# Moving the last sequence's gated experts into the scans of the next block

## The chip, the cores and the metric

The kernel runs on one core of a Trainium2 chip as one launch. The metric is the device time in microseconds, as the median of several executions. TensorE (PE), VectorE (DVE), ScalarE (ACT), GpSimd (POOL) and SyncE (SP, which here issues most DMAs) work from queues of their own and wait for each other by semaphores.

## The reference

Eight sequences of 512 tokens of 128 features (float32) go through four layers, each an attention part and a feed-forward part with a residual. The change touches where the third layer's feed-forward part (gated experts) meets the fourth layer's attention part (a state-space scan). What matters:

```python
# L2 ffn: 32 experts of 64 units, 4 of them chosen for each token
gates = sigmoid(xt @ expert_sel.T); gate_full = gates of the 4 largest, else 0
scores = relu(einsum('nd,edf->nef', xt, keys)) * gate_full[:, :, None]
out = einsum('nef,efv->nv', scores, values)          # added to x
# L3 attn: for each of 16 heads, 8 channels and 48 states
h = exp(dt_t * A) * h + (dt_t * u_t) * b_t           # along the 512 tokens
y_t = sum over states of h * c_t
```

After the scan there are an output projection, a gated MLP (`silu(gate) * up`, then `down`), and the last layer's feed-forward part with spiking units.

## The kernel before

`NB = 8` sequences, `S = 512` tokens, `P = D = 128`. The residual `X[b]` of all sequences stays in SBUF (four tiles of 128 tokens each). The function `l2_attn_l3_attn` (from L1072) holds both stages that matter.

*Expert stage* (L1626 to L1667). For each sequence `b` it runs 16 steps `j` of two experts. A step multiplies the normalised, transposed sequence `xT` with two experts' keys into PSUM (`key`, L1644), VectorE takes the maximum with 0 and multiplies with the gates (`act`, L1648, gates spread over 64 partitions each by DMA, `fetch_gates`, L1397), and three steps later TensorE multiplies with the values and accumulates (`acc`, L1622). After 16 steps `give_back` (L1408) copies, transposes and adds the sum to `X[b]` and takes the statistics for the next norm. Beside these steps run, one piece at each step, the generators in `side`: `route` (router of the next sequence), `banded` (attention of the one after) and twice `prepare`. In the last sequence's 16 steps, the fifth also issues the first loads of the scans (`fetch`, `fetch_dt`, L1656 to L1660).

*Scan stage* (L1860 to L1911). For each sequence there are four row blocks `q` and three state groups `g`: a *group* in the text is one (b, q, g), of which a sequence has 12. A group does, twice (`j` = 0, 1): two matmuls `bx` (L1879) from `gx`, an exponential `a` on ScalarE (L1885), and the scan `h` on VectorE (L1890). `bx` has two PSUM buffers, `a` four buffers. The group's output matmuls `Z` (`give`, L1690) follow one group later. `gx` is loaded by four DMAs (L1313, three buffers) and multiplied in place with `xk` by GpSimd (`products`, L1335). Beside the groups, one piece each, run the generators in `side`: `prepare(b + 2)` (L1227: norm, convolution, step size with a polynomial for log(1+z) on GpSimd, L1271 to L1292), `project(b - 1)` (L1703: projection and MLP, with GpSimd's L1727 and L1732 ahead of the transposes at L262) and late in the stage `layer_3b`. They share two PSUM buffers (`mm_tile`, L1101).

The order of the text is not quite the order of the queues: when the program is built, the tile framework puts the instructions of each engine into one list, which the engine then follows. What is called "the built program" below is this list.

Of the kernel before, what the change touches and what calls it, by code (L numbers as in the profile page):

```python
# [16 lines left out]
F32 = mybir.dt.float32  # L17
BF16 = mybir.dt.bfloat16
AF = mybir.ActivationFunctionType
ALU = mybir.AluOpType  # L20
# [3 lines left out]
P = 128  # L24
NB = 8
S = 512
C = S // P
D = 128
# [39 lines left out]
def eight_layers(ctx: ExitStack, tc: tile.TileContext, w: dict, out: bass.AP):  # L68
    nc = tc.nc

    const = ctx.enter_context(tc.tile_pool(name="const", bufs=1))
# [40 lines left out]
    X = [xpool.tile([P, C, D], F32, tag=f"x{b}", name=f"x{b}") for b in range(NB)]  # L112
# [9 lines left out]
    later = []  # L122
# [6 lines left out]
    def square(name, put=load):  # L129
        return put(name, [P, P], w[name])  # L130
# [43 lines left out]
    f1_sg = load_later("L1_ffn_shared_gate_w", [P, 512], w["L1_ffn_shared_gate_w"])  # L174
# [3 lines left out]
        w["L1_ffn_shared_down_w"].rearrange("(k p) d -> p k d", p=P),  # L178
    )

    a2 = {k: square(f"L2_attn_{k}", load_later) for k in ("WQ", "WK", "WV")}
    f2_sel = load_later("L2_ffn_expert_sel", [P, 32], w["L2_ffn_expert_sel"])
    f2_k = load_later("L2_ffn_keys", [P, 32, 64], w["L2_ffn_keys"].rearrange("e d f -> d e f"))
    f2_v = load_later(
# [55 lines left out]
    def cols(c):  # L240
        return slice(c * P, (c + 1) * P)

    def stats(b, mv, x=None):

        x = X[b] if x is None else x
        for c in range(C):
            st = small.tile([P, 6], F32, tag="bn", name="bn", bufs=4)
            nc.vector.bn_stats(st, x[:, c, :])  # L248
            nc.vector.bn_aggr(mv[:, b * C + c, :], st)
# [822 lines left out]
    def l2_attn_l3_attn():  # L1072
# [15 lines left out]

        E = 32
        J = E // 2  # L1090
        G = 3
        Q = 4
        with ExitStack() as es:
# [7 lines left out]
            def mm_tile():  # L1101
                return ps.tile([P, S], F32, tag="mm", name="mm")
# [24 lines left out]
            def step(gens):  # L1127
                for g in list(gens):
                    if next(g, None) is None:
                        gens.remove(g)  # L1130
# [93 lines left out]
            x1 = {}  # L1224
            rows = {}

            def prepare(b, fine=False):  # L1227
# [5 lines left out]
                nc.gpsimd.tensor_tensor(rr, rr, mv3[:, tiles(b), 1], ALU.mult)  # L1233
                nc.gpsimd.tensor_scalar(rr, rr, 1e-6, None, ALU.add)
                nc.gpsimd.tensor_tensor(rr, rr, minus_half[:, 0:C], ALU.pow)
                xn = work.tile([P, C, D], F32, tag="x1", name="x1", bufs=NB)
                normal(b, mv3, r, xn)
                x1[b] = xn
                yield True
# [98 lines left out]
            with ExitStack() as es2:  # L1338
# [25 lines left out]
                def route(b):  # L1364
                    r = rstd_of(mv2, b, b == 0)
                    yield True
                    xn = ffn.tile([P, C, D], F32, tag="xn", name="xn")
                    normal(b, mv2, r, xn)
                    yield True
                    xT = ffn.tile([P, S], F32, tag="xT", name="xT")  # L1370
                    flipped(xn, mm_four(), xT)
                    yield True
                    lp = mm_four()[:, :, 0:E]
                    for c in range(C):
                        nc.tensor.matmul(lp[:, c, :], xT[:, cols(c)], f2_sel, start=True, stop=True)
                    gt = ffn.tile([P, C, E], F32, tag="gt", name="gt")
                    nc.scalar.activation(gt, lp, AF.Sigmoid)
                    yield True
                    full = first_max(gt, False)
                    for k in range(1, 4):  # L1380
                        yield True
                        oh = first_max(gt, k == 3)
                        nc.vector.tensor_tensor(full, full, oh, ALU.add)
                    yield True
                    mm = mm_four()
                    for c in range(C):
                        nc.tensor.transpose(mm[0:E, c, :], full[:, c, :], ident)
                    gT = ffn.tile([E, S], F32, tag="gT", name="gT", bufs=1)
                    nc.scalar.copy(gT, mm[0:E].rearrange("p c t -> p (c t)"))
                    gd = dram.tile([E, S], F32, tag="gates", name="gates", bufs=3)  # L1390
                    nc.sync.dma_start(gd, gT)
                    ready[b] = xT, gd
                    yield True
# [229 lines left out]
                    if j == J - 1:  # L1623
                        side.append(give_back(b, acc))

                for b in range(NB):  # L1626
                    xT = ready[b][0]
                    if b < NB - 1:
                        side.append(route(b + 1))
                    if b < NB - 2:  # L1630
                        side.append(banded(b + 2))
                    if b < NB - 3:
                        gather(b + 3)
                    acc = ps2.tile([P, S], F32, tag="acc", name="acc", bufs=2)
                    for j in range(J):
                        if j % 2 == 0:
                            m = 8 * b + j // 2 + 3
                            if m < 8 * NB:
                                while m // 8 not in ready:
                                    step(side)  # L1640
                                fetch_gates(m // 8, m % 8)
                            gate = spread.pop((b, j // 2))
                        key = ps2.tile([P, S], F32, tag="key", name="key", bufs=3)
                        nc.tensor.matmul(  # L1644
                            key, f2_k[:, 2 * j : 2 * j + 2, :], xT, start=True, stop=True
                        )
                        act = ffn.tile([P, S], F32, tag="act", name="act", bufs=5)
                        nc.vector.scalar_tensor_tensor(  # L1648
                            act, key, 0.0, gate[:, j % 2, :], ALU.max, ALU.mult
                        )  # L1650
                        if len(sums) > 2:
                            add_up()
                        sums.append((b, j, act, acc))
                        if j == 4 and b in (NB - 5, NB - 3):
                            side.append(prepare((b - NB + 5) // 2, True))
                        if j == 4 and b == NB - 1:  # L1656
                            nc.vector.tensor_copy(late, act[:, 0:2])
                            fetch(0, 0)
                            fetch_dt(0, 0)
                            fetch(0, 1)  # L1660
                        if j == 12 and b == NB - 1:
                            products(0, 0)
                        step(side)
                while sums:
                    add_up()
                while side:
                    step(side)  # L1667


            with ExitStack() as es2:  # L1670
# [32 lines left out]
                def project(b, zx):  # L1703
# [59 lines left out]
                    given.add(b)  # L1763
                    yield True

                order = [(b, q) for b in range(NB) for q in range(Q)]

                inputs = {}
# [2 lines left out]
                def layer_3b(b, tail):  # L1771
# [51 lines left out]
                            yield True  # L1823
                    y = o.rearrange("p c d -> p (c d)")
                    if b < NB - 1:
                        y = work.tile([P, S], F32, tag="x1", name="x1", bufs=NB)
                        nc.scalar.copy(y, o.rearrange("p c d -> p (c d)"))
                    inputs[b] = y
                    yield True
# [27 lines left out]
                    nc.gpsimd.dma_start(out[b].rearrange("(c p) d -> p c d", p=P), X[b])  # L1857
                    yield True

                side = []  # L1860
                n = 0
                for b in range(NB):
                    if b < NB - 2:
                        side.append(prepare(b + 2))
                    for q in range(Q):
# [7 lines left out]
                        for g in range(G):  # L1873
                            hs = []
                            for j in range(2):
# [16 lines left out]
                                    bx.rearrange("p r t -> p (r t)"), 0.0, ALU.mult, ALU.add,  # L1892
                                )
                                hs.append(h)
                            made.append((b, q, g, hs, xk))
                            if len(made) > 1:
                                give()
# [87 lines left out]
```

## Time and profile before

| | us |
|---|---|
| median of 3 runs (lowest, highest) | 1713.37 (1712.08, 1717.24) |
| the profiled execution, its own time | 1725.08 |
| its span from first to last instruction | 1723.3 |
| busy: TensorE, VectorE, ScalarE, GpSimd | 1470.0, 1206.9, 796.6, 677.8 |
| experts of the last sequence, from the first of its value matmuls to the last | 1098.1 to 1122.8 |
| first scan starts | 1129.8 |
| granted TensorE clock, mean | 0.935 |

An engine's row in the timeline gives start and duration in us, engine, line, operation, tiles, shapes and, in brackets, the idle time before and who ended it. A matmul of float32 appears as two records. In a row of stretches, each engine has its busy time and (in brackets) its number of instructions, followed by TensorE's clock, the DMA engines' busy share and GB/s. In the waits, each line says which line of which engine waited for which, for how long in total, how often, and the longest. The chain of waits is followed back from the last instruction.

### The profile page before, as it was taken

Reading aid. Unit: us, or ns where it says so; the run is one execution under the profiler, and the core shown is the slowest. Engines: PE = TensorE matmul, PEld = TensorE weight load, DVE = VectorE, ACT = ScalarE, POOL = GpSimd, SP = SyncE. Lnnn points to the kernel's source line nnn. Section 1 sums busy time; section 2 is a strip of 40 time slices with the busy share of each in tenths; the row PEclk is TensorE's granted clock in tenths of the full one; section 3 lists DMA queues with packets and bytes.
Section 4 is the critical chain, followed back from the end, with each engine's and each line's share of the span. In section 5 each row is a group of like instructions: output and inputs, shape, how many; then the busy total and the mean of one; then the engine's idle time right before and its main releaser. Section 6 shows DMA issues by size and latency. Waiting matters only on the chain.

```text
span 1723.3 us, 22463 instructions
## 1 busy us (share of the span) xinstructions
PE 1470.0 (85%) x8060; PEld 651.2 (38%) x8061; DVE 1206.9 (70%) x2374; ACT 796.6 (46%) x1158; POOL 677.8 (39%) x728
## 2 busy tenths in 40 slices
PE   5978898899888868988999896977888888888887
PEld 2322333334344435644555453422222222233335
DVE  7688666655654444357775764589899999988765
ACT  3655655555454423353223230055555565565634
POOL 4754344443321140211213318135645645712750
PEclk8999899999899889988999898999899999999988
DMA  7991000000000022304544653634444444443201
GB/s 270 384 342 34 1 1 13 7 13 13 13 19 19 13 99 78 95 10 109 124 116 118 134 126 95 151 80 129 124 127 128 133 129 125 131 117 95 61 13 31
DMA packets 94224, 164.69 MB, mean 96 GB/s; under 512 B 10848, under 2 KB 36960, under 8 KB 90016
## 3 DMA queue, kind: packets, MB, share of 16 engines
q1 hardware_dynamic: 89392, 151.97, 31.4%
q0 software_dynamic: 3568, 9.18, 1.7%
q10 hardware_dynamic: 1152, 2.10, 0.4%
q8 instruction: 64, 1.05, 0.3%
q14 instruction: 48, 0.39, 0.1%
HBM read 110.27 MB, written 52.95 MB: 95 GB/s over the span
## 4 chain that ended last, share of the span: by engine, by line
PE 43%; DVE 28%; issue 10%; POOL 7%; ACT 5%; DMA 5%; SPq 1%; DVEq 0%; POOLq 0%; ACTq 0%
DVE h L1890 11%; PE key L1644 5%; PE acc L1622 5%; PE bx L1879 3%; DMA gx<-du_d 2%; PE mm L262 2%; PE sT L568 2%; DVE mf L547 2%; PE o L591 2%; PE sc L536 1%; PE gu L369 1%; PE gu L1055 1%; DMA gate<-gates 1%; DVE zx L1698 1%; PE Z L1690 1%
## 5 line engine op out<-in xcount | busy, mean ns | idle before, releaser
L1890 DVE TENSOR_TENSOR_SCAN h<-a,bx 128x1024 f32<-128x1024 f32 x192 | 426.9, 2269 | 29.2 <-PE bx L1879 27.7
L1885 ACT ACTIVATE a<-dr,nA 128x1022 f32<-128x1022 f32 x192 | 219.4, 1146 | 221.2 <-DVE h L1890 221.0
L1879 PE MATMUL bx<-gx,wb 64*128 64x512 f32 x768 | 220.2, 666 | 61.3 <-DVE h L1890 59.2
L1335 POOL TENSOR_TENSOR gx<-gx,xk 128x1024 f32<-128x1024 f32 x32 | 75.4, 2357 | 226.0 <-DMA gx<-du_d 194.3
L1644 PE MATMUL key<-xT,L_ffn_keys 128*128 128x512 f32 x256 | 136.4, 615 | 22.9 <-DVE act L1648 22.9
L1879 PEld LDWEIGHTS bx<-gx,wb 64*128 64x128 f32 x768 | 64.8, 195 | 195.1 <-DVE h L1890 149.8
L1622 PE MATMUL acc<-act,L_ffn_values 128*128 128x512 f32 x256 | 132.7, 602 | 0.0
L1648 DVE SCALAR_TENSOR_TENSOR act<-key,gate 128x512 f32<-128x512 f32 x128 | 86.5, 685 | 47.8 <-PE key L1644 34.6
L1690 PE MATMUL Z<-h,wc 64*32 64x512 f32 x1536 | 110.3, 628 | 0.1
L547 DVE TENSOR_REDUCE mf<-sm 128x8 f32<-128x1024 f32 x64 | 76.1, 1211 | 42.5 <-POOL sm L543 42.4
L577 POOL TENSOR_SCALAR_AFFINE_SELECT eT<-eT 128x1024 f32<-128x1024 f32 x64 | 68.9, 1099 | 78.7 <-ACT eT L575 78.7
L543 POOL TENSOR_SCALAR_AFFINE_SELECT sm<-sm 128x1024 f32<-128x1024 f32 x64 | 69.4, 1098 | 71.2 <-ACT sm L542 70.9
L1433 POOL DMA_INDIRECT back<-f_out,back_at x32 | 30.8, 964 | 155.7 <-DVE bn L248 139.3
L542 ACT COPY sm<-sc 128x1024 f32<-128x1024 f32 x64 | 62.5, 1014 | 54.7 <-PE sc L536 40.6
L1410 ACT COPY oT<-acc 128x512 f32<-128x512 f32 x8 | 4.7, 587 | 159.2 <-PE acc L1622 159.2
L575 ACT ACTIVATE eT<-sT 128x1024 f32<-128x1024 f32 x64 | 62.0, 1021 | 28.0 <-PE sT L568 27.9
L1644 PEld LDWEIGHTS key<-xT,L_ffn_keys 128*128 128x128 f32 x256 | 47.1, 195 | 73.2 <-issue 36.2
L1622 PEld LDWEIGHTS acc<-act,L_ffn_values 128*128 128x128 f32 x256 | 49.1, 193 | 60.0 <-issue 60.0
L536 PE MATMUL sc<-kb,qT 32*128 32x512 f32 x256 | 58.9, 724 | 10.0 <-ACT sm L542 4.1
L248 DVE BATCH_NORM_STATS2 bn<-x 128x6 f32<-128x128 f32 x224 | 56.1, 272 | 4.8 <-DMA x<-in_L_attn_hidden_states 4.0
L1116 POOL TENSOR_TENSOR rstd<-rstd,minus_half 128x4 f32<-128x4 f32 x27 | 28.0, 1040 | 80.0 <-DVE rstd L1115 79.8
L568 PE MATMUL sT<-qT,kb 32*128 32x512 f32 x256 | 55.2, 655 | 4.5 <-ACT sm L542 2.9
(482 smaller groups left out, 3006.4 us busy)
## 6 DMA issues: line engine op xcount, KB each, us to landing
f_in<-zeros SPq DMA_DIRECT2D x10, 3584.0 KB
gate<-gates SPq DMA_DIRECT2D x128, 256.0 KB
dr<-dt_d SPq DMA_DIRECT2D x32, 1024.0 KB
gx<-du_d SPq DMA_DIRECT2D x128, 128.0 KB
xk<-xh_d SPq DMA_DIRECT2D x32, 256.0 KB
wide<-in_L_ffn_experts SPq DMA_DIRECT2D x1, 3072.0 KB
xg<-f_in SPq DMA_DIRECT2D x48, 64.0 KB
f_out<-ys SPq DMA_DIRECT2D x12, 256.0 KB
```

The lines of the kernel that those rows point to most:

```text
L536: nc.tensor.matmul(halves[q // 2][:, 4 * (q % 2) : 4 * (q % 2) + 4, :], qT[quad(q), cols(c)], kb[quad(q)], start=True, stop=True,)
L543: nc.gpsimd.affine_select(out=sm, in_=sm, compare_op=ALU.is_ge, fill=-1e30, base=0, pattern=[[0, 8], [-1, P]], channel_multiplier=1,)
L547: nc.vector.tensor_reduce(mf[:, c, 2 * i : 2 * i + 2], sm.rearrange("p (q r) k -> p q r k", q=2), AX.X, ALU.max, negate=True,)
L568: nc.tensor.matmul(halves[q // 2][:, q % 2, :], lhs[quad(q), r, :], rhs[quad(q)], start=(k == 0), stop=(k == 1),)
L1335: nc.gpsimd.tensor_tensor(gx, gx, xk.unsqueeze(1).to_broadcast([P, 2, S]), ALU.mult)
L1622: nc.tensor.matmul(acc, f2_v[:, j, :], act, start=(j == 0), stop=(j == J - 1))
L1644: nc.tensor.matmul(key, f2_k[:, 2 * j : 2 * j + 2, :], xT, start=True, stop=True)
L1648: nc.vector.scalar_tensor_tensor(act, key, 0.0, gate[:, j % 2, :], ALU.max, ALU.mult)
L1690: nc.tensor.matmul(zs[q][32 * j : 32 * j + 32, i, :], wcf[half, g, :], hs[j // 2][half, j % 2, :], start=(g == 0), stop=(g == G - 1),)
L1879: nc.tensor.matmul(bx[:, k, :], wbf[half, g, :], gx[half, j, :], start=True, stop=True,)
L1885: nc.scalar.activation(a[:, :, 1:], dr[:, 2 * j : 2 * j + 2, 1:], AF.Exp, scale=nA[:, q, g : g + 1],)
L1890: nc.vector.tensor_tensor_scan(h.rearrange("p r t -> p (r t)"), a.rearrange("p r t -> p (r t)"), bx.rearrange("p r t -> p (r t)"), 0.0, AL ...
```

## The change

The expert stage now runs over seven sequences. The last sequence's route is still computed there; its 16 steps become the generator `last_experts`, of which one piece is run in each group of the scans, between the group's two `bx` (34 pieces, so they end in the third block). The pieces are: one matmul with the keys, Relu by ScalarE, the product with the gates by GpSimd; and after each second step, two pieces of four small matmuls with the values, each for half of the tokens, a copy to SBUF by ScalarE and an addition to `X` by GpSimd. Gates come by two DMAs a step. To find room in SBUF, the pieces reuse weights that are no longer needed (`f1_sg`, `f1_su` for the activations, `f1_sd` for `xT`, two of the three squares of `a2` for the copy), and `x1` has one buffer less. The scans' first loads move to the steps of sequence 6 (`LAST - 1`).

```diff
-    a2 = {k: square(f"L2_attn_{k}", load_later) for k in ("WQ", "WK", "WV")}
+    a2_all = const.tile([P, 3, P], F32, tag="L2_attn_W", name="L2_attn_W")
+    a2 = {}
+    for i, k in enumerate(("WQ", "WK", "WV")):
+        a2[k] = a2_all[:, i]
+        later.append((a2[k], w[f"L2_attn_{k}"]))
...
+        LAST = NB - 1
...
-                xn = work.tile([P, C, D], F32, tag="x1", name="x1", bufs=NB)
+                xn = work.tile([P, C, D], F32, tag="x1", name="x1", bufs=NB - 1)
...
-                    xT = ffn.tile([P, S], F32, tag="xT", name="xT")
+                    if b == LAST:
+                        xT = f1_sd.rearrange("p k d -> p (k d)")
+                    else:
+                        xT = ffn.tile([P, S], F32, tag="xT", name="xT")
...
-                for b in range(NB):
+                for b in range(LAST):
...
-                            if m < 8 * NB:
+                            if m < 8 * LAST:
...
-                        if j == 4 and b == NB - 1:
+                        if j == 4 and b == LAST - 1:
...
-                        if j == 12 and b == NB - 1:
+                        if j == 12 and b == LAST - 1:
...
+                last_xT, last_gates = ready[LAST]
...
+                def last_experts():
+
+                    acts = f1_sg, f1_su
+                    part = a2_all[:, 0:2]
+                    gates = {}
+
+                    def fetch_gate(j):
+                        t = scan.tile([P, S], F32, tag="gate", name="gate")
+                        for k in range(2):
+                            nc.sync.dma_start(
+                                t[64 * k : 64 * k + 64],
+                                last_gates[2 * j + k : 2 * j + k + 1, :].to_broadcast([64, S]),
+                            )
+                        gates[j] = t
+
+                    fetch_gate(0)
+                    yield True
+                    for j in range(J):
+                        if j + 1 < J:
+                            fetch_gate(j + 1)
+                        act = acts[j % 2]
+                        key = mm_tile()
+                        nc.tensor.matmul(
+                            key, f2_k[:, 2 * j : 2 * j + 2, :], last_xT, start=True, stop=True
+                        )
+                        nc.scalar.activation(act, key, AF.Relu)
+                        nc.gpsimd.tensor_tensor(act, act, gates.pop(j), ALU.mult)
+                        yield True
+                        if j % 2 == 0:
+                            continue
+                        for at in (slice(0, 2), slice(2, 4)):
+                            o = mm_tile()[:, 0 : 2 * D].rearrange("p (c d) -> p c d", c=2)
+                            for c in range(2):
+                                for i in range(2):
+                                    nc.tensor.matmul(
+                                        o[:, c, :], acts[i][:, cols(at.start + c)],
+                                        f2_v[:, j - 1 + i, :], start=(i == 0), stop=(i == 1),
+                                    )
+                            nc.scalar.copy(part, o)
+                            nc.gpsimd.tensor_tensor(X[LAST][:, at], X[LAST][:, at], part, ALU.add)
+                            yield True
+                    stats(LAST, mv3)
+                    yield True
...
-                        y = work.tile([P, S], F32, tag="x1", name="x1", bufs=NB)
+                        y = work.tile([P, S], F32, tag="x1", name="x1", bufs=NB - 1)
...
-                side = []
+                side, between = [], [last_experts()]
...
+                                if j == 0:
+                                    step(between)
```

## The prediction

> **What bounds the kernel now.** I read the page's chain of waits first, then the busy time by stretches around the stage that the change takes away, then the waits of the scan stage, then the timelines of GpSimd and TensorE there.
>
> The chain by lines (its shares are of the whole span):
>
> ```profile
> PE 43%; DVE 28%; issue 10%; POOL 7%; ACT 5%; DMA 5%; SPq 1%; DVEq 0%; POOLq 0%; ACTq 0%
> DVE h L1890 11%; PE key L1644 5%; PE acc L1622 5%; PE bx L1879 3%; DMA gx<-du_d 2%; PE mm L262 2%; PE sT L568 2%; DVE mf L547 2%; PE o L591 2%; PE sc L536 1%; PE gu L369 1%; PE gu L1055 1%; DMA gate<-gates 1%; DVE zx L1698 1%; PE Z L1690 1%
> ```
>
> Two stages concern us: in the experts TensorE carries the chain (`key`, `acc`), in the scans VectorE does (`h`). Busy time by stretches (us, then each engine's busy time and count, TensorE's clock, DMA):
>
> ```profile
> 1098.00:1122.70 24.70, 24.70 (x61) 10.84 (x59) 12.15 (x29) 0.48 (x4) 8.05 (x4) 1.00 0.70 173
> 1162.00:1178.00 16.00, 11.02 (x76) 2.68 (x76) 16.00 (x8) 8.02 (x7) 15.15 (x14) 1.00 0.44 111
> 1386.00:1450.00 64.00, 54.97 (x356) 17.66 (x356) 61.93 (x43) 36.42 (x44) 36.08 (x32) 0.95 0.48 130
> ```
>
> The first is the last sequence's experts: TensorE has no gap. The third is one block (12 groups) of scans: VectorE busy 61.9 of 64 us, TensorE 55. The second holds only scans on VectorE, while GpSimd is busy 15.15 of 16 us: that row decides the forecast. Who waits in the scans (total us, times, longest):
>
> ```profile
> PE bx L1879 <- DVE h L1890: 59.2, 55, 5.5
> DVE h L1890 <- PE bx L1879: 27.7, 25, 5.5
> PE mm L262 <- POOL u L1732: 10.1, 4, 4.9
> ```
>
> TensorE mostly waits for VectorE, so there is room on it; the third row is a case where TensorE waits for something that GpSimd has in its queue behind other work.
>
> **The change, part by part.** Sums are made against the profiled execution (span 1723.3, its own time 1725.08 us); that is 0.7% above the median 1713.37, so differences are carried over as they are.
>
> *Removed: the stage, -27.4 us.* In its timeline a `key` and an `acc` matmul follow each other every 1.715 us; 16 pairs are 27.4 us, with TensorE at 100%. What follows (copy, transposes, statistics, first scan at 1129.8) stays, now with sequence 6. The stage also hid the first loads and products of the scans: first issue 1103.2, third product done 1116.5, so 13.3 us. They move to the fifth of 16 steps of sequence 6, with 12 x 1.715 = 20.6 us left: 0. The 16 gate products leave VectorE (0.685 each), which was not the bound there: 0.
>
> *Added, as sums.* TensorE: 16 `key` matmuls of 0.86 and 64 small ones at 0.26 (eight records of L1719 take 1.06), about 30 us in 34 steps, one a group. ScalarE: 16 Relu at 0.58 and 16 copies of 256 columns (between 0.30 for 128 and 0.58 for 512; 0.40): 16 us, while it is busy 36 of 64. GpSimd: 16 products at 1.28 and 16 additions of half the size at 0.65: 31 us, while it is busy 36 of 64. SyncE: 32 gate loads of 128 KB at 0.57 us of issue, in a queue that waits most of the time. No engine but TensorE comes near its limit.
>
> *Does a step fit on TensorE?* In a plain group the scans start 2.18 us apart; two `bx` (1.13 each) and `Z` (1.09) make 3.35 of 4.36 us. A step of 0.86 to 1.0 us fills the gap of 1.0. In blocks with the side matmuls, 55 + 12 x 0.93 = 66 of 64 us: at most 2.5 us a block. Where TensorE is behind already (VectorE waits 1.5 us for it at 1149) a step costs its full length. Packed `bx` are cheaper (eight records in 1.99 us, not twice 1.13), which may take all of it back: 0 to 10 us, I take 4.
>
> *Port and tables.* GpSimd's new reads run beside the scans. The Trainium skill (SBUF — State Buffer, section "Who interferes with whom") says that a VectorE instruction with two SBUF inputs contends with a GpSimd instruction that reads SBUF, one blocking the other. That would speak against the move: if it held for the scans, up to GpSimd's 31 us would be lost. But a scan has one input in PSUM (`bx`), and the 176 scans of 1128 to 1600 last 2253 to 2289 ns, whether GpSimd is busy (1158 to 1181) or idle (1185 to 1200). I follow the row: 0. Relu and copy add no table load: the built program has none new, and Relu of L1803 runs among the Exp without one.
>
> *The waits that it adds.* Each pair of experts ends in matmuls (two steps, "O" here) that need both gate products, and these now stand in GpSimd's queue. The built program puts them, in the block where the queue is fullest, like this (line numbers of the changed kernel; L1276 to L1290 are the polynomial of `prepare`, L1801 the gate products of experts j=2 and j=3):
>
> ```
> L1276 z   L1278 lp   L1283 two   L1284 lp
> L1801 act(j=2) <- act, gate
> L1287 lp  L1283 two  L1284 lp  L1287 lp  L1283 two  L1284 lp  L1287 lp
> L1283 two  L1284 lp  L1287 lp  L1290 lp
> L1801 act(j=3) <- act, gate
> ```
>
> The same polynomial in the trace of before:
>
> ```profile
> 1158.34 1.04 POOL L1271 TENSOR_TENSOR z<-z 128x512 f32<-128x512 f32 x1 [5.34 <-ACT z L1265]
> 1160.15 0.62 POOL L1278 TENSOR_SCALAR two<-z 128x512 f32<-128x512 f32 x1
> 1160.85 1.29 POOL L1279 TENSOR_TENSOR lp<-lp,z 128x512 f32<-128x512 f32 x1
> 1162.22 1.28 POOL L1282 TENSOR_TENSOR lp<-lp,two 128x512 f32<-128x512 f32 x1
> 1163.58 0.62 POOL L1278 TENSOR_SCALAR two<-z 128x512 f32<-128x512 f32 x1
> 1172.41 1.27 POOL L1282 TENSOR_TENSOR lp<-lp,two 128x512 f32<-128x512 f32 x1
> 1173.63 2.38 POOL L1335 TENSOR_TENSOR gx<-gx,xk 128x1024 f32<-128x1024 f32 x1
> ```
>
> A two-input operation takes 1.36 us from start to start, a one-input one 0.69. From 1158.3: four operations to 1162.2, j=2 to 1163.5, then 8 x 1.36 + 3 x 0.69 = 13.0 us, j=3 done at 1177.8. TensorE reaches O at about 1163.2; it is in order, and the next `bx` stands behind O, so the scan due at 1167.4 starts at 1177.8 + 1.0 + 1.1 = 1179.9: 12.5 us lost by VectorE. This comes three times: for j=9 one more operation stands before the product (O's side matmuls give some back: 11.4), for j=15 a `gx` product of 2.4 as well (13.8). Together 37.7. After such an idle time TensorE is slow too:
>
> ```profile
> 1220.99 1.11 PE L262 MATMUL mm<-ident,u 128*128 128x128 f32 x4 [4.94 <-POOL u L1732]
> 1222.03 3.79 PE L1879 MATMUL bx<-gx,wb 64*128 64x512 f32 x8
> ```
>
> 3.79 against 1.99 us, 1 to 2 us each time. I take 40. Below: 0, if the list were not kept; but GpSimd shows no passing: at 1281.1 it has sat 8.57 us before a `gx` product, while the next in its list (L1727) had its input from VectorE at 1273.5. Above: 3 x 16.
>
> Twice a `gx` product, which waits for its load (launched 1170.9, done 1184.2 to 1186.5), stands before j=4, 5 and j=10, 11: 1186.5 + 2.7 = 1189.2 against O at 1182.7, minus 1 us of slack, 5.5; the second by its own rows (1247.8) 1 to 5. I take 6 (0 to 12). At two block starts an addition (L1814) stands behind such a product, the copy of the second half waits for its only buffer, and a matmul of `prepare` for the copy's PSUM: 3 each beyond the wait there now (-2 to 6): 6.
>
> Sum: -27.4 + 4 + 40 + 6 + 6 = +28.6, so 1713.4 + 28.6 = 1742 us.
>
> **Rivals.**
> *The steps fit (faster).* TensorE's gap of 1 us a group takes each step, GpSimd is busy only 36 of 64 us and reaches each product before O. Then only the matmuls' own cost, at most 10, stands against 27.4: 1713.4 - 27.4 + 10 = 1696. For it: the 59.2 us of TensorE's waits. Against: the list above. It decides at the waits' sum: under 23 us (27.4 - 4) the kernel is faster, so the three long ones would have to be under 4 us each. Chance 0.14.
>
> *Only the short waits.* The polynomial starts later, or O is late by its other inputs, so that the long waits shrink to 4 us each: -27.4 + 4 + 12 + 6 + 6 = +0.6, 1714. Chance 0.12 (faster 0.04, same 0.05, slower 0.03).
>
> *GpSimd's list bounds the scans:* 1742, own range 1722 to 1765 by the bounds above. Chance 0.74.
>
> **The numbers.** About 0.3% (5 us) is what a measurement of this kernel can tell from no change. Faster 0.14 + 0.04 = 0.18, same 0.05, slower 0.74 + 0.03 = 0.77. The range runs from 1700 (it leaves out most of the first rival) to 1765.
>
> **What would show it.** Right: O's matmuls (L1809) wait for GpSimd (L1801) three times by 10 us or more, `h` waits for `bx` by about 60 us more, GpSimd is busy at those moments with L1284 and L1287; the 27 us of the stage are gone and the first scan starts about 1102. The scans stay at 2.26 us; if they lengthen, the port does contend. Wrong: O waits little, and the first three blocks last near 64 us each; then the first rival holds.

## The result and the profile after

| | before | after |
|---|---|---|
| median of 4 runs (lowest, highest), us | 1715.30 (1712.08, 1718.50) | 1772.18 (1766.77, 1775.57) |
| span of the profiled execution, us | 1723.3 | 1769.2 |
| busy: TensorE, VectorE, ScalarE, GpSimd, us | 1470.0, 1206.9, 796.6, 677.8 | 1492.0, 1201.2, 809.2, 707.6 |
| first `key` of sequence 6 to first `zx`, us | 86.1 | 64.2 |
| first `zx` to twelfth `zx` (blocks 0 to 2), us | 176.4 | 247.7 |

The ratio of the times is 1.0329 (95% interval 1.0294 to 1.0364): slower, as forecast, but by 57 us where 28.6 were forecast; 1772 lies above the range. Lines below are the changed kernel's: `h` L1943, `bx` L1932, `Z` L1699; of the steps `key` L1797, Relu L1800, gate product L1801, value matmuls ("O") L1809, copy L1813, addition L1814; the polynomial L1276 to L1290, `gx` product L1340.

The last two rows of the table cut the kernel where the change acts. A `zx` (L1707) ends each quarter of a block, so its rows in VectorE's timeline give the pace; the first cut starts at the `key` matmul that follows a wait of 14.5 us in both kernels. The differences, -21.9 and +71.3, give +49.4; what lies ahead and behind gives -3.5, and the spans differ by 45.9. (The first scan starts at 1107.5, where about 1102 was forecast.)

The chain of waits of the page after, by engine and by line:

```profile
PE 44%; DVE 25%; POOL 10%; issue 9%; ACT 6%; DMA 5%; SPq 1%; POOLq 0%; DVEq 0%; ACTq 0%
DVE h L1943 8%; PE key L1652 4%; PE acc L1630 4%; PE bx L1932 4%; DMA gx<-du_d 3%; PE mm L266 2%; PE sT L572 2%; PE Z L1699 2%; DVE mf L551 2%; PE gu L373 2%; PE sc L540 1%; PE o L595 1%; PE gu L1059 1%; POOL lp L1284 1%; PE kq L771 1%
```

GpSimd's share rose from 7 to 10%, with `lp`, a line of the polynomial, among its lines; `h` fell from 11 to 8%. The waits of blocks 0 to 2 (total us, times, longest) say who waits, before and after:

```profile
DVE h L1890 <- PE bx L1879: 10.5, 9, 5.5
PE bx L1879 <- DVE h L1890: 29.7, 26, 5.5
```

```profile
DVE h L1943 <- PE bx L1932: 70.8, 22, 13.3
PE bx L1932 <- DVE h L1943: 13.0, 9, 3.2
PE mm L1809 <- POOL L_ffn_shared_up_w L1801: 32.1, 6, 11.8
PE mm L1809 <- POOL L_ffn_shared_gate_w L1801: 10.3, 3, 3.7
```

TensorE used to wait for VectorE; now VectorE waits for TensorE, and TensorE's O for the gate products. The stretches show it too: VectorE, with 61.9 of 64 us busy before, has 45.82 and 44.53, at a TensorE clock of 0.85 and 0.89 (0.98 and 1.00 in the same two stretches of e22 below, which has the same matmuls without these waits); once the steps are over (third row) all is as before.

```profile
1112.00:1176.00 64.00, 51.50 (x294) 16.82 (x294) 45.82 (x24) 28.99 (x34) 34.33 (x35) 0.85 0.39 109
1176.00:1240.00 64.00, 52.25 (x286) 19.09 (x286) 44.53 (x24) 31.52 (x45) 31.37 (x28) 0.89 0.42 112
1386.00:1450.00 64.00, 56.02 (x374) 17.91 (x372) 62.54 (x43) 37.35 (x49) 36.24 (x33) 0.95 0.47 128
```

One of the long waits, from GpSimd's timeline (the products of j=2 and j=3 and what stands between, cut) and from TensorE's:

```profile
1142.37 1.27 POOL L1801 TENSOR_TENSOR L_ffn_shared_gate_w<-L_ffn_shared_gate_w,gate 128x512 f32<-128x512 f32 x1
1143.61 1.27 POOL L1287 TENSOR_TENSOR lp<-lp,two 128x512 f32<-128x512 f32 x1
...
1155.07 1.26 POOL L1290 TENSOR_TENSOR lp<-lp,z 128x512 f32<-128x512 f32 x1
1156.28 1.26 POOL L1801 TENSOR_TENSOR L_ffn_shared_up_w<-L_ffn_shared_up_w,gate 128x512 f32<-128x512 f32 x1
```

```profile
1145.32 0.49 PE L1809 MATMUL mm<-L_ffn_values,L_ffn_shared_gate_w 128*128 128x128 f32 x2
1157.60 0.79 PE L1809 MATMUL mm<-L_ffn_values,L_ffn_shared_up_w 128*128 128x128 f32 x2 [11.79 <-POOL L_ffn_shared_up_w L1801]
...
1159.18 2.08 PE L1932 MATMUL bx<-gx,wb 64*128 64x512 f32 x4
```

ScalarE had the Relu of j=3 done at 1143.2; the product started 13 us later because eleven operations of the polynomial were ahead of it. The second half of O and then `bx` stood behind it on TensorE, and `bx` then took 2.08 and not 1.13 us. The scan that waits starts 12.19 us late; for j=9 it is 12.44 and for j=15 13.31 us.

On the gain side, the last steps of sequence 6: two rows of GpSimd, two of VectorE and two of TensorE.

```profile
1081.34 2.35 POOL L1340 TENSOR_TENSOR gx<-gx,xk 128x1024 f32<-128x1024 f32 x1 [2.28 <-DMA gx<-du_d]
1084.62 2.46 POOL L1340 TENSOR_TENSOR gx<-gx,xk 128x1024 f32<-128x1024 f32 x1 [0.94 <-DMA gx<-du_d]
```

```profile
1081.39 2.44 DVE L1361 TENSOR_TENSOR oh<-oh_eq,oh_f 128x128 f32<-128x128 f32 x1
1084.80 2.43 DVE L1352 TENSOR_TENSOR oh_eq<-gt,oh_m 128x128 f32<-128x128 f32 x1
```

```profile
1087.88 1.12 PE L1652 MATMUL key<-xT,L_ffn_keys 128*128 128x512 f32 x2 [2.06 <-DVE act L1656]
1093.11 0.60 PE L1395 MATMUL mm<-ident,oh 128*32 128x128 f32 x4 [2.38 <-DVE oh L1391]
```

The same comparisons of the route take 0.28 to 0.29 elsewhere. These two began just after a moved `gx` product and ended with it, and TensorE then waited for VectorE.

### The profile page after: what moved, and what is told of

Read it like the earlier page. It is cut to its first block, busy times and chain, and to the rows that moved or that the text cites. A ratio compares the mean times of both kernels' runs of the same rounds, so it can differ in the third digit from the quotient of the medians.

```text
span 1769.2 us, 22733 instructions
## 1 busy us (share of the span) xinstructions
PE 1492.0 (84%) x8152; PEld 662.4 (37%) x8153; DVE 1201.2 (68%) x2357; ACT 809.2 (46%) x1189; POOL 707.6 (40%) x760
## 4 chain that ended last, share of the span: by engine, by line
PE 44%; DVE 25%; POOL 10%; issue 9%; ACT 6%; DMA 5%; SPq 1%; POOLq 0%; DVEq 0%; ACTq 0%
DVE h L1943 8%; PE key L1652 4%; PE acc L1630 4%; PE bx L1932 4%; DMA gx<-du_d 3%; PE mm L266 2%; PE sT L572 2%; PE Z L1699 2%; DVE mf L551 2%; PE gu L373 2%; PE sc L540 1%; PE o L595 1%; PE gu L1059 1%; POOL lp L1284 1%; PE kq L771 1%
## 5 line engine op out<-in xcount | busy, mean ns | idle before, releaser
L1943 DVE TENSOR_TENSOR_SCAN h<-a,bx 128x1024 f32<-128x1024 f32 x192 | 428.0, 2270 | 91.7 <-PE bx L1932 86.2
L1932 PE MATMUL bx<-gx,wb 64*128 64x512 f32 x768 | 226.2, 675 | 44.8 <-DVE h L1943 43.9
L1340 POOL TENSOR_TENSOR gx<-gx,xk 128x1024 f32<-128x1024 f32 x32 | 75.5, 2358 | 218.2 <-DMA gx<-du_d 182.2
L1652 PE MATMUL key<-xT,L_ffn_keys 128*128 128x512 f32 x224 | 121.8, 626 | 22.4 <-DVE act L1656 22.4
L1932 PEld LDWEIGHTS bx<-gx,wb 64*128 64x128 f32 x768 | 64.4, 196 | 171.2 <-DVE h L1943 124.6
L1630 PE MATMUL acc<-act,L_ffn_values 128*128 128x512 f32 x224 | 117.7, 610 | 0.0
L1699 PE MATMUL Z<-h,wc 64*32 64x512 f32 x1536 | 113.2, 643 | 1.1 <-DVE h L1943 1.1
L1656 DVE SCALAR_TENSOR_TENSOR act<-key,gate 128x512 f32<-128x512 f32 x112 | 75.8, 683 | 38.4 <-PE key L1652 33.2
L547 POOL TENSOR_SCALAR_AFFINE_SELECT sm<-sm 128x1024 f32<-128x1024 f32 x64 | 69.4, 1099 | 71.6 <-ACT sm L546 71.3
L1652 PEld LDWEIGHTS key<-xT,L_ffn_keys 128*128 128x128 f32 x224 | 41.5, 198 | 66.2 <-issue 31.8
L1630 PEld LDWEIGHTS acc<-act,L_ffn_values 128*128 128x128 f32 x224 | 43.6, 197 | 53.5 <-issue 53.5
L881 POOL DMA_INDIRECT f_in<-xr,to x32 | 33.2, 1037 | 61.0 <-DMA f_in<-xr,to 34.6
```

The costliest lines, as they stand in the source:

```text
L547: nc.gpsimd.affine_select(out=sm, in_=sm, compare_op=ALU.is_ge, fill=-1e30, base=0, pattern=[[0, 8], [-1, P]], channel_multiplier=1,)
L1340: nc.gpsimd.tensor_tensor(gx, gx, xk.unsqueeze(1).to_broadcast([P, 2, S]), ALU.mult)
L1630: nc.tensor.matmul(acc, f2_v[:, j, :], act, start=(j == 0), stop=(j == J - 1))
L1652: nc.tensor.matmul(key, f2_k[:, 2 * j : 2 * j + 2, :], xT, start=True, stop=True)
L1656: nc.vector.scalar_tensor_tensor(act, key, 0.0, gate[:, j % 2, :], ALU.max, ALU.mult)
L1699: nc.tensor.matmul(zs[q][32 * j : 32 * j + 32, i, :], wcf[half, g, :], hs[j // 2][half, j % 2, :], start=(g == 0), stop=(g == G - 1),)
```

## The experiments

The theory after the result: GpSimd's list is most of the loss (long waits and waits at `gx` products), the moved products take a part of the gain by the port, and TensorE's steps cost something by themselves. The rival: TensorE or GpSimd simply has too much to do, and the order in a list does not matter. Other groups of runs had medians of the kernel before of 1719 to 1724, so kernels are compared by their ratio to it. A is the first cut of the table above, B the second (profiled execution; the kernel before has 86.1 and 176.4). e1, e5, e17, e18 and e22 leave out a part of the computation and serve only to take the time apart.

| kernel | median | ratio (95% interval) | A | B |
|---|---|---|---|---|
| the change | 1772.2 | 1.0329 (1.0294, 1.0364) | 64.2 | 247.7 |
| e1 no experts of the last sequence | 1703.4 | 0.9918 (0.9882, 0.9953) | 64.6 | 180.9 |
| e22 TensorE's matmuls alone, no gate loads | 1717.8 | 0.9987 (0.9967, 1.0008) | 62.9 | 192.8 |
| e17 the same, with gate loads | 1726.5 | 0.9994 (0.9963, 1.0024) | 65.6 | 207.0 |
| e18 as e17, step after both `bx` | 1724.4 | 0.9999 (0.9969, 1.0028) | 65.2 | 197.2 |
| e5 no gate products | 1729.8 | 1.0057 (1.0032, 1.0081) | 63.2 | 203.9 |
| e12 gates and additions on VectorE | 1727.3 | 1.0052 (1.0026, 1.0077) | 65.8 | 207.9 |
| e3 gates on VectorE | 1738.9 | 1.0113 (1.0088, 1.0139) | 64.6 | 216.7 |
| e4 three gates on VectorE | 1738.4 | 1.0087 (1.0043, 1.0131) | 65.4 | 221.7 |
| e10 polynomial held in its groups | 1745.8 | 1.0146 (1.0103, 1.0190) | 64.4 | 228.1 |
| e9 all of GpSimd's list held | 1780.9 | 1.0344 (1.0300, 1.0387) | | 222.3 |
| e2 late first loads | 1762.1 | 1.0246 (1.0194, 1.0299) | 58.6 | 251.1 |
| e20 e12 and late first loads | 1723.9 | 1.0009 (0.9982, 1.0036) | 59.7 | 207.1 |
| e21 e20, step after both `bx` | 1722.1 | 0.9971 (0.9948, 0.9994) | 59.8 | 203.2 |
| e23 the same again | 1725.0 | 1.0035 (1.0008, 1.0062) | 60.1 | 205.9 |
| e13 e20, 34 steps over 60 groups | 1729.0 | 1.0046 (1.0015, 1.0077) | 58.9 | |
| e14 e20, groups 5 to 11 of a block | 1737.8 | 1.0086 (1.0056, 1.0117) | 59.0 | |
| e16 e14, step after both `bx` | 1727.6 | 1.0040 (1.0015, 1.0066) | 59.9 | |
| e15 e10, late loads, 60 groups | 1754.7 | 1.0174 (1.0142, 1.0207) | 59.2 | |

(e9 has no wait of 14.5 us at which A could start; where the steps go on after the twelfth `zx`, B is left out.)

**e1, the gain alone.** The loop of `last_experts` runs zero times; the statistics stay.

```diff
-                    fetch_gate(0)
                     yield True
-                    for j in range(J):
+                    for j in range(0):
```

> Leaves out the last sequence's experts (neither in a stage nor as steps); all else is as in the changed kernel. It gives the gain side alone. By the prediction the stage is worth 27.4 us: 1715.3 - 27.4 = 1688. By what the trace of the changed kernel shows (first scan at 1107.5 and not at 1102: two GpSimd gx products at 1081.3 and 1084.6 lie beside two VectorE operations that take 2.43 us in place of 0.28, and TensorE waits 2.06 + 2.38 us right after): some 22 us, 1693, and the same two long operations are there again.

A ratio of 0.9918 is 14 us less than before, and A is 21.5 us shorter, not 27.4. Two long comparisons are there again. The forecast of the gain falls. B is 4.5 us longer than before although no step runs: VectorE waits 7.3 us once for a GpSimd operation of `project` (L1741), a wait that neither the kernel before nor the change has.

**e2, the moved products away from the route.** Loads start at step 12 of sequence 6, the product at step 14.

```diff
-                        if j == 4 and b == LAST - 1:
+                        if j == 12 and b == LAST - 1:
...
-                        if j == 12 and b == LAST - 1:
+                        if j == 14 and b == LAST - 1:
```

> As the changed kernel, but the scans' first loads start at step 12 of sequence 6 and not at step 4 (the first product at step 14), so that the gx products no longer lie beside the last route's comparisons on VectorE. If the port holds these back (2.43 us in place of 0.28, twice, in the changed kernel), they are 0.28 again, TensorE's waits of 2.06 and 2.38 go, and the first scan starts some 4 us earlier: 1772 - 4 = 1768, provided that the third product (10 us later) does not become the last. If the loads come too late, +2 to +6.

The comparisons are short again, in VectorE's timeline and with the product in GpSimd's:

```profile
1080.80 0.29 DVE L1361 TENSOR_TENSOR oh<-oh_eq,oh_f 128x128 f32<-128x128 f32 x1
```

```profile
1092.21 2.35 POOL L1340 TENSOR_TENSOR gx<-gx,xk 128x1024 f32<-128x1024 f32 x1 [16.42 <-DMA gx<-du_d]
```

A is 58.6, which is 27.5 under before: the full 16 x 1.715 (the later versions with late loads have 58.9 to 60.1). From the first `key` of sequence 6 to the transposes of its `give_back` it takes 33.6 us, against 38.8 to 41.2 in the ten kernels with early loads where both rows can be read. The ratio fell by 0.0083, 14 us; A says 5.6 of it, and the rest isn't settled (B is even 3.4 longer, and e21 and e23 below show that two groups of runs of one kernel can differ by 0.0064).

**e3, e4, e5, the gate products away from GpSimd**, all of them, three of them, or left out.

```diff
-                        nc.scalar.activation(act, key, AF.Relu)
-                        nc.gpsimd.tensor_tensor(act, act, gates.pop(j), ALU.mult)
+                        nc.vector.scalar_tensor_tensor(act, key, 0.0, gates.pop(j), ALU.max, ALU.mult)
```

e4 does this for j in (3, 9, 15) only; e5 keeps the Relu and drops the product.

> All 16 gate products by one VectorE operation from PSUM (maximum with 0, times gate) in place of Relu on ScalarE and product on GpSimd. GpSimd's list as cause: the long waits (37.9 us) and the short ones at gx products (15.9) go, 16 x 0.69 = 11 us of VectorE are added: 1772 - 54 + 11 = 1729. If the additions L1814, still in GpSimd's list behind the polynomial, hold the copy's only buffer and so the PSUM buffers, half of the waits come back: about 1750. TensorE as cause (it is simply full): no gain, 1772 to 1783.

> Only the products of j=3, 9 and 15 by VectorE, the other 13 stay on GpSimd. By the prediction's mechanism the three long waits (12.2 + 12.4 + 13.3) go for 3 x 0.69: 1772 - 36 = 1736. If what stands next in GpSimd's list (the additions L1814 behind the polynomial) then holds the PSUM buffers instead: 1755 to 1765. If TensorE is full: 1772.

> Leaves out the multiplication with the gates in the last sequence's steps (Relu writes what the value matmuls read; gates are loaded and not used). What is left is the cost of TensorE's steps, ScalarE and the additions. GpSimd's products as cause of 54 of the 71 us: 1772 - 54 = 1718. Additions take over half of it: 1745. TensorE full: 1765 to 1772.

e4 came to the expected 1736 within its interval: three operations moved, 26 us less in B. This points to the list, not the amount; e10 below tests it without moving anything to another engine. e3 lies between its first two cases and e5 between its own: with the products gone, the additions are next. In e5, GpSimd and TensorE:

```profile
1159.73 2.34 POOL L1340 TENSOR_TENSOR gx<-gx,xk 128x1024 f32<-128x1024 f32 x1 [6.86 <-DMA gx<-du_d]
1162.03 1.26 POOL L1297 TENSOR_TENSOR du<-dt,xt 128x512 f32<-128x512 f32 x1
...
1164.42 0.73 POOL L1814 TENSOR_TENSOR x<-x,L_attn_W 128x256 f32<-128x256 f32 x1
```

```profile
1165.62 2.08 PE L1797 MATMUL mm<-L_ffn_shared_down_w,L_ffn_keys 128*128 128x512 f32 x2 [10.30 <-ACT L_attn_W L1813]
```

The addition of the first half stands behind the polynomial and a `gx` product; ScalarE's copy of the second half waits for its only buffer, 16.4 us, and the next `key` for the PSUM buffer that the copy holds.

**e10 and e9, the same instructions in another order on GpSimd.** e10 pins the polynomial's one-input operation behind what the text has ahead of it; e9 keeps all of GpSimd's list in the scan stage in the order of the text.

```diff
-                    nc.gpsimd.tensor_scalar(two, z, LOG1P[k + 1], LOG1P[k], ALU.mult, ALU.add)
+                    piece = nc.gpsimd.tensor_scalar(two, z, LOG1P[k + 1], LOG1P[k], ALU.mult, ALU.add)
+                    if not fine:
+                        tc.keep_in_program_order(piece)
```

> The same instructions; only the polynomial's one-input operations are held in GpSimd's list behind what the text has ahead of them, so that the products of j=3, 9 and 15 stand behind some 5 us of polynomial and not 13. List order as cause: three waits of 12 to 13 us become some 4 us, 1772 - 26 = 1746; the gx waits (15.9) stay. Amount of work as cause: 1772.

> The same instructions as the changed kernel; only GpSimd's list in the scan stage is kept in the order of the text, where three operations of the polynomial stand in a group and never more than these ahead of a gate product. If the place in the list is the cause: the three waits of 12 to 13 us shrink to under 4 each, 1772 - 27 = 1745, less still if the waits at gx products shrink too (1735); if a gx product that waits for its load then stands ahead of products and additions more often: 1755. If the amount of GpSimd's or TensorE's work is the cause: 1772.

e10 gave 1745.8 where 1746 was expected: nothing is removed, B falls by 19.6. In the traces TensorE, VectorE and ScalarE do the same instructions in the same order as in the change; only GpSimd's order differs. The scans late by 12.2 to 13.3 us are late by 5.46, 4.38 and 5.48, and the waits of its O (L1813 there) are

```profile
PE mm L1813 <- POOL L_ffn_shared_up_w L1805: 9.4, 6, 5.1
PE mm L1813 <- POOL L_ffn_shared_gate_w L1805: 8.2, 3, 2.9
```

This leaves nothing of the rival "amount of work" for the long waits. e9 missed in its total, not in the waits at stake. In blocks 0 to 2 it is better still (222.3; O waits 8.8 us for L1801 in all), but blocks 3 to 6 take 71.6, 71.3, 84.9 and 85.8 us where the change has 63.1, 62.7, 63.3 and 72.0, 52.5 more: a list in the order of the text makes others late, as these waits of 1320 to 1600 show:

```profile
DVE rstd L1120 <- POOL u L1127: 28.1, 2, 22.6
DVE x L1127 <- POOL rstd L1121: 15.8, 2, 7.9
```

e9 is not a clean test, though: in its trace the orders of VectorE and TensorE differ from the change's too. Thus it also gains ahead of the scans: its first `zx` comes at 1109.4 and not at 1127.3. The wait of 14.5 us before sequence 6, which every other kernel has, the kernel before too, is gone. It is a wait of the same kind: VectorE's norm waits for a small GpSimd operation (`rstd`) that stands among the polynomial's, and the `act` that TensorE needs stands behind the norm on VectorE. In e9 `rstd` comes no earlier, but the norm has a later place in VectorE's list. The norm in the kernel before, and in e9:

```profile
1059.72 1.28 DVE L1122 TENSOR_SCALAR x<-x,mv,rstd 128x128 f32<-128x128 f32 x1 [18.06 <-POOL rstd L1116]
```

```profile
1073.42 0.35 DVE L1127 TENSOR_SCALAR x<-x,mv,rstd 128x128 f32<-128x128 f32 x1 [0.94 <-POOL rstd L1121]
```

No kernel here joins this gain of 18 us with the held polynomial of e10.

**e12, nothing of the steps on GpSimd or ScalarE.** As e3, and the addition by VectorE straight from PSUM.

```diff
-                            nc.scalar.copy(part, o)
-                            nc.gpsimd.tensor_tensor(X[LAST][:, at], X[LAST][:, at], part, ALU.add)
+                            nc.vector.tensor_tensor(X[LAST][:, at], X[LAST][:, at], o, ALU.add)
```

> Gate products by one VectorE operation from PSUM and additions by VectorE from PSUM too: nothing of the steps is left on GpSimd or ScalarE, TensorE's steps are unchanged. VectorE gets 16 x 0.69 + 16 x about 0.4 = 17 us. Without the steps the kernel took 1703; if GpSimd's list is the whole of the loss beyond TensorE's share (some 15 us by its small waits): 1703 + 17 + 15 = 1735 at most, 1722 if TensorE's share lies beside VectorE's. If TensorE is full by itself: 1750 and more.

1727.3, between 1722 and 1735. The 32 operations take 0.67 and 0.40 us each, 17.1 us on the engine that bounds the scans, and still the kernel is 45 us faster than the change.

**e17, e18, e22, TensorE's steps alone.** Nothing reads the matmuls' results; e18 has the step behind both `bx` (`if j == 1`), e22 has no gate loads.

> Of the last sequence's experts only TensorE's matmuls are left, in the same 34 steps (no Relu, no gates, no copy, no addition; the value matmuls read fixed data). Beside the kernel without steps (1703) it gives TensorE's own cost: by the forecast 4 for the steps and 6 for the block starts, 1713; by what is left over when VectorE's own 17 us are taken from the version with all on VectorE, 14, thus 1717; if a step fits in TensorE's gap of 1 us, 1703.

> As the one before, but each step stands after the two bx of its group and not between them. If the broken pairs (twice 1.13 in place of eight records in 1.99, 0.27 us a group) are what makes TensorE late: 34 x 0.27 = 9 us less TensorE time and 5 to 9 us less in all, 1708 to 1712. If the length of the steps beside the side work is the cause: 1715 to 1717.

> TensorE's matmuls of the last sequence's experts alone, in their 34 steps, and the gate loads are left out too (with Relu, gates, copies and additions). Ratio to the kernel before: 0.992 for no steps at all, 0.999 for matmuls and idle gate loads. If the loads in SyncE's queue were the cause: 0.993. If TensorE's own time is: 0.998 to 1.000; by the forecast's 10 us, 0.998.

Over e1 the three are 0.0069 to 0.0081 dearer, 12 to 14 us, not much more than the 0.0064 by which e21 and e23 differ; but all three agree, and the traces do too: in B of e22 VectorE is idle 12.7 us more than before (23.8 against 11.1), and busy 3.7 us more (169.0 against 165.3), as the last sequence's statistics and a normalisation now fall into this cut. So a step does not fit in the gap, and the gate loads that are never read are not the cause. Nor do the broken pairs of `bx` show in the ratio: e18 is not under e17 (in the profiled executions its B is 9.8 shorter, which the ratio does not bear out). In the profiled executions e17's and e18's B are longer than e22's; there gate loads that nobody reads wait 20.5 and 20.9 us in SyncE's queue (a scale load `dr` kept ScalarE 11.1 us in e17), which the ratios don't bear out either. In e22 `h` waits for `bx` 18 times, none long:

```profile
DVE h L1936 <- PE bx L1925: 17.4, 18, 2.3
```

The longest, of 2.3 us, stand beside `prepare`'s convolution (3.7 us of TensorE without a break) and `project`: there TensorE has no gap, as the forecast said, and a step costs its length.

**e13 to e16, other groups for the steps.** With late loads; e13, e14 and e16 have gates and additions on VectorE, e15 on GpSimd with the held polynomial.

```diff
-                                if j == 0:
+                                at = 12 * b + 3 * q + g
+                                if j == 0 and at * 34 // 60 != (at + 1) * 34 // 60:
                                     step(between)
```

e14 has `if j == 0 and 3 * q + g > 4`, e16 the same with `j == 1`.

> Gates and additions on VectorE, the late first loads, and the 34 steps spread over 60 groups (34 of 60 have one) and not over the first 34. With steps in each of the first 34 groups and early loads it was 1727. Late loads should give 9 (first products are away from the route's comparisons). If TensorE is over full in the groups with other side work, a share of the 24 us that h waits for bx goes with the steps that now fall in other groups, some 6: 1727 - 9 - 6 = 1712. If spreading does nothing: 1718.

> As the one before, but steps only in groups 5 to 11 of each block (35 in five blocks), which have least other work on TensorE. If TensorE's small waits come from steps beside the norm's transposes, the convolution and the projection at the block's start, most of the 24 us goes: 1727 - 9 - 12 = 1706. If they come from wherever a step stands: 1718.

> Gates and additions stay on GpSimd and Relu and copy on ScalarE as in the changed kernel, with the polynomial's operations held in their groups, the late first loads, and the steps over 60 groups. The held polynomial alone gave 1746; late loads 9 less, 1737. If products and additions still wait behind the polynomial and behind gx products, no more comes: 1730 to 1740. If half as many steps a block meet them half as often: 1720.

> As with groups 5 to 11 only, but the step stands after the second bx and not between the two, so that two bx can go without a break (eight records took 1.99 us in the kernel before, twice 1.13 with a step between). If that packing counts, 0.27 us x 34 = up to 9 us less on TensorE, of which little is on the path: 0 to 3 us under the version between. If the gate operation then comes later and the value matmuls wait for it: 1 to 5 us more.

e13, e14 and e15 missed, by 17, 32 and 15 to 35 us; e16 came 10 us under e14 where 0 to 3 were expected. Spreading moves the waits. In e14 the twelfth `zx` comes 197.7 us after the first (207.1 in e20, where all steps are done by then), but block 4 takes 80.1 us against 63.5 in e20: six steps are in it, and `rstd` waits 4.4 us for GpSimd's norm of `layer_3b` (the rest of the 16.6 isn't traced). In block 1 a scan waits 8.3 us because `project`'s transposes wait for an operation of GpSimd (L1741) that stands behind a `gx` product. Why e14 and e16 are that far apart isn't settled.

**e20, e21, e23, what is left of the gain.** e12 with late loads; e21 and e23 with the step behind both `bx`.

> Gates and additions on VectorE, steps in the first 34 groups, and the late first loads. With early loads 1727; the sequence before the scans takes 39 to 41 us from its first key matmul to its last transposes with early loads and 34 with late ones, so 1727 - 5.6 = 1721. If the late third product takes it back: 1727.

> As the one before with the step after the two bx. If packing counts: 1721 - 5 = 1716, level with the kernel before; if VectorE's gate operation, later in its list, makes the value matmuls wait: 1721 to 1726.

> The version with gates and additions on VectorE, the late first loads and steps after the two bx once more, in five rounds: 0.997 of the kernel before, as in its first run (0.9948 to 0.9994), if that was no chance; 1.000 if it was.

e20 is level with before. e21 looked 0.3% faster and e23, the same kernel, 0.35% slower; the two intervals don't overlap, so they understate how groups of runs differ, and together they say: no difference. No version here that computes the whole result beats the kernel before. e20's cuts say why: it gains 26.4 us in A and loses 30.7 in B, where TensorE's steps (16.4 in e22) and VectorE's 32 operations (17.1 us in e12) are added.

## Why the prediction was right in direction and wrong in size

Point by point, forecast against the profiled executions:

| step | forecast | measured | from |
|---|---|---|---|
| removed stage | -27.4 | -27.5 | A of e2 |
| first loads and products moved | 0 | +5.6 | A of the change less A of e2 |
| TensorE's steps | +4 | +12.7 | VectorE's idle time in B, e22 less before |
| VectorE's work that moved into the scans | none | +3.7 | its busy time in B, e22 less before |
| long waits of O | +40 | +37.9 | three gaps before `h` |
| waits of O at `gx` products | +6 | +15.9 | gaps of 5.46, 6.20, 4.23 |
| block starts | +6 | +1.1 | what is left of B |
| sum | +28.6 | +49.4 | |

The last row but one is a remainder, so it is no test that the sum comes out. The main mechanism held. The sum failed at three terms that were too small: the moved products (0 for 5.6), the waits at `gx` products (6 for 15.9) and TensorE's steps (4 for 12.7). By luck two terms were too large, the block starts by 5 and the long waits by 2, which hid a part of that.

*The long waits* were right: three, for j=3, 9 and 15, behind L1284 and L1287 as the built program had it; 12.2, 12.4 and 13.3 us against 12.5, 11.4 and 13.8 (TensorE's own waits there are 11.8, 8.9 and 9.8, so two of them stay under the 10 us that I had named as a sign; `h` waits for `bx` by 60 us more, as I had named). e4 and e10 show the cause. *The stage's own 27.4* was right as well, and so was the remark that slow TensorE follows a wait.

*"They move to the fifth of 16 steps: 0"* failed. I looked whether the loads have time, not what runs beside the products there. (The 1116.5 that I took for the third product's end is the second's; the third ended at 1122.5, 19.3 us after the first issue, which still fits into 20.6.) It is the rule of the Trainium skill (SBUF — State Buffer, "Who interferes with whom") that I had weighed for the scans only: a VectorE instruction with two SBUF inputs contends with a GpSimd instruction that reads SBUF, and one waits for the other. The scans have one input in PSUM and did stay (mean 2270 ns, 2269 before). The route's comparisons have two in SBUF: 2.43 in place of 0.28 us. Rule and row agree there, e2 takes the two long rows away, and the term is 5.6 us.

*"Twice a `gx` product stands before O: 6"* was right in mechanism and mis-sized. It came three times, before j=4, 6 and 12 (not at 10), and I left out the slow clock after it. GpSimd's and TensorE's rows at the first:

```profile
1177.33 2.35 POOL L1340 TENSOR_TENSOR gx<-gx,xk 128x1024 f32<-128x1024 f32 x1 [11.09 <-PE bx L1932]
1179.64 1.26 POOL L1801 TENSOR_TENSOR L_ffn_shared_gate_w<-L_ffn_shared_gate_w,gate 128x512 f32<-128x512 f32 x1
```

```profile
1180.96 0.80 PE L1809 MATMUL mm<-L_ffn_values,L_ffn_shared_gate_w 128*128 128x128 f32 x2 [3.64 <-POOL L_ffn_shared_gate_w L1801]
...
1183.76 2.08 PE L1932 MATMUL bx<-gx,wb 64*128 64x512 f32 x4
```

A wait of 3.64 us becomes 5.46 for the scan: O and `bx` behind it are slower (0.80 and 2.08 for 0.49 and 1.13). The load was issued at 1166.1, as its buffer comes free from a `bx` that the long wait had delayed: waits breed waits. A second path does the same, and I had only noted that SyncE's queue waits most of the time: a gate load needs the buffer that a gate product gives free, and stands in the queue until then, with the scans' loads behind it. SyncE's waits in blocks 0 to 2:

```profile
SPq L1784 <- POOL L_ffn_shared_gate_w L1801: 72.0, 7, 15.7
SPq L1784 <- POOL L_ffn_shared_up_w L1801: 28.6, 3, 11.4
```

From 1168.5 to 1180.9 SyncE issues nothing for this reason. How much of the 15.9 us comes from it no run here separates.

*"0 to 10 us, I take 4" for TensorE's steps* was mis-sized: 12.7 us by e22's trace, 12 to 14 by the ratios. The bound "at most 2.5 us a block" averaged over a block in which groups with the convolution have no gap at all. That packed pairs would matter does not show in e18's ratio. *The block starts* were too large: an addition did stand behind a `gx` product at both, but TensorE's matmul (L1266) waited for the copy (L1813) only once, 0.95 us.

The terms miss 49.4 - 28.6 = 20.8 us. The other 7 or so up to 57 lie in carrying a difference of profiled executions over to medians "as they are": the profiled execution of before was 10 us above its own median (1725.08, 1715.3), that of the change was not. About 5 of these 10 us lie behind the twelfth `zx`, where the change does nothing: 399.2 us to the end, against 394.2 in the change and 390.4 to 396.1 in the thirteen other kernels whose steps are over by then (e9 apart). With medians of 1719 to 1724 for the kernel before in the later groups, the difference would be 48 to 53.

Of the rivals, "the steps fit" fell with e22 and "only the short waits" with the three long ones.

## What to carry to other kernels

When work moves onto an engine with time to spare, read the place of each moved instruction in that engine's list, with the measured durations of what stands ahead, and follow who is in order behind it: here GpSimd was busy 34 of 64 us, and still a product stood behind 13 us of another sequence's polynomial; moving three of 16 products away took the ratio from 1.0329 to 1.0087. Ask it of the kernel before as well: there a wait of 14.7 us is of the same kind. Ask of each moved piece, of the loads and first products too, what it will run beside at its new place. A gap that is an average over a block is not a gap in each group.

## What the hardware showed that I had not expected

VectorE's two-input comparison beside a GpSimd product does not slow down, it stops: started 0.05 us after the product, it ends 0.14 us after it, 2.44 us for 0.28. Each of the eleven kernels with early loads has two such rows among the route's two-input operations, of 1.84 to 2.44 us. A one-input VectorE operation did so too. In e2 the `rstd` (L1120) of the norm, which takes 0.17 us elsewhere, and the GpSimd product beside it:

```profile
1096.40 2.28 DVE L1120 TENSOR_SCALAR rstd<-mv 128x4 f32<-128x4 f32 x1
```

```profile
1096.17 2.36 POOL L1340 TENSOR_TENSOR gx<-gx,xk 128x1024 f32<-128x1024 f32 x1 [1.61 <-DMA gx<-du_d]
```

Seven of the eight kernels with late loads have such a `rstd`, of 1.14 to 2.28 us, that ends 0.15 to 0.17 us after its product. The Trainium skill (SBUF — State Buffer, "Who interferes with whom") counts tensor_scalar among the operations that can take the pair of ports that VectorE shares with GpSimd, which these rows agree with; the trace does not show in which mode it ran.
